# The end of the last image in a deformable-attention and bottleneck kernel: rows dealt by a product, a convolution by chunks, and depthwise steps on two engines

## The chip, the cores and the metric

The kernel runs on one core of a Trainium2 chip. The metric is the device time of one execution in microseconds (us). Three runs of the kernel before gave 3307.5, 3316.93 and 3306.41 us; the median is 3307.5 us. All data are 32-bit floats.

The engines are named as in the profile: PE (TensorE, matrix products, with PEld for its weight loads), DVE (VectorE), ACT (ScalarE), POOL (GpSimd) and SP (SyncE, which here only issues DMAs).

## What is computed

Eight images of 512 channels and 64x64 pixels pass through two layers. Each layer normalises its input over 32 groups of channels and adds its output to its input.

```python
# layer 0: deformable attention, 8 heads of 64 channels
q = einsum('oc,bchw->bohw', w_q, gn(x))
off = tanh(w_off2 @ gelu(q[..., ::4, ::4] * w_off1 + b_off1)) * 4
k, v = split(w_kv @ grid_sample_bilinear(q, grid + off))     # 16x16 = 256 keys
out = softmax((q * 0.125) @ k.T) @ v
x = x + w_out @ out + b_out

# layer 1: bottleneck
y = conv_w @ gn(x) + conv_b                       # 512 -> 32 channels
y = depthwise 3x3, stride 2 (y) + dw_b            # 64x64 -> 32x32
y = fc2_w @ (fc1_w @ y + fc1_b) + fc2_b           # 1024 -> 256 -> 1024 pixels
y = depthwise transposed 3x3, stride 2 (y) + de_b # 32x32 -> 64x64
x = x + out_w @ y + out_b                         # 32 -> 512 channels
```

## The kernel before

An image is held as 8 tiles of 512 pixels; a tile has 4 chunks of 128 channels on 128 partitions. The loop at L1101 goes over 256 rounds (image, tile, chunk) and 6 more. In a round, PE computes logits of the next round, weighted values and sums of exponentials of this one, and the output projection of the round 6 back (`LAG`), so that projection, residual add and statistics trail the attention. Work of layer 1 of the image before and of layer 0 of the next one is woven in by generators. All of it stands under a manual schedule: on each engine, the order of the code is the order of the instructions.

What happens behind the last attention round, in the code's names:

- `sum_exps` (L618) adds up the exponentials with a 0/1 matrix into the PSUM tile `pn`. `invert` (L637) takes the reciprocal `rn` on DVE (L641), and four small DMAs on SP (L647) copy rows of `rn` to other partitions[...].
- `scale_two` (L650) spreads a row of `rn` over its head's partitions by a shuffle (L654) and multiplies the weighted values with it (L656).
- `project_out` (L664) multiplies a tile with `wout`, 128x64 column tiles in pairs, 8 products for one chunk of output (L670). DVE then adds bias and residual (L677) and takes the statistics of the chunk (L680).
- `load_residual` (L658) and `store` (L682) are DMAs on SP.
- After the 6 trailing rounds, `layer1_last` (L991) runs `layer1` (L733) for the last image with nothing beside it: statistics over all chunks by `group_stats` (L164), whose power -0.5 is on POOL (L185); the convolution weights `cw` scaled by it (L746); the convolution `py` (L753), where each of four row blocks of an image uses 32 columns of PE; the same weights applied to the means (`pb`, L771), for the bias; copies by ACT into the padded map `y` in `wbuf` (L765); the bias added by DVE (L780); three row copies between blocks (L782); nine taps of the first depthwise step on DVE (L798, L800); transposes `pz`, the two linear steps `ph`, `pht`, `pu`; the map `u` (L864); the 18 tap operations of `upsample` on DVE (L884, L886) into `v`.
- `project_last` (L952) forms 32 output products of 128x512 in up to 6 PSUM banks at a time. For 24 of them DVE adds them to the residual (L983); for 8, ACT evicts (L980) and POOL adds (L981). Each is stored by its own DMA of 256 KB on SP (L986).

PSUM pools: `ps_s` has two buffers of two banks, `ps_a` the two banks `pa` and `pn`, `ps_mm` two banks.

Of the kernel before, what the change touches and what calls it, by code (L numbers as in the profile page):

```python
# [8 lines left out]
F32 = mybir.dt.float32  # L9
# [7 lines left out]
P = 128  # L17
# [32 lines left out]
def kernel(  # L50
# [45 lines left out]
    def spot(b, k):  # L96
        j = region[b]
        k %= NT + 1
        return spares[j] if k == 0 else regions[j][:, :, (k - 1) * TP : k * TP]
# [7 lines left out]
    def out_tile(b, t):  # L107
        return spot(b, t - 1)
# [40 lines left out]
    def col(k, n=1):  # L149
        return vec[:, k : k + n]  # L150
# [4 lines left out]
    def drain(*gens):  # L155
        for gen in gens:
            for _ in gen:
                pass
# [502 lines left out]
            xs[place[b]][:, oc : oc + n, t * TP : (t + 1) * TP],  # L661
        )

    def project_out(b, t, oc, st):  # L664

        ao, xt = q_tile(b, t), out_tile(b, t)
        pp = ps_mm.tile([P, TP], F32, tag="mm", name=f"pp_{b}_{t}_{oc}")
        for hp in range(NCC):
            for r in (0, DH):
                nc.tensor.matmul(  # L670
                    pp[r : r + DH, :],
                    wout[:, hp, oc * P + r : oc * P + r + DH],
                    ao[:, hp, :],
                    start=(hp == 0),
                    stop=(hp == NCC - 1),
                )
        nc.vector.scalar_tensor_tensor(  # L677
            xt[:, oc, :], pp, col(V_BOUT + oc), xt[:, oc, :], ALU.add, ALU.add
        )
        nc.vector.bn_stats(st[:, oc, t, :], xt[:, oc, :])  # L680
# [4 lines left out]
    def attention_max(b, t):  # L685

        qt = q_tile(b, t)
        for hp in range(NCC):
# [40 lines left out]
                    )  # L729
            nc.scalar.copy(qt[:, hp, :], pa)  # L730


    def layer1(b, st, project, place, v):  # L733

        w2 = {}
        for half in range(2):
# [4 lines left out]
                    fc2_wT[oc * P : (oc + 1) * P, half * 2 * NK : (half + 1) * 2 * NK],  # L741
                )

        gs = yield from group_stats(st, 1, b)
        cw = small.tile([P, NCC, CB], F32, tag="cw", name=f"cw_{b}")
        nc.vector.tensor_mul(cw, convw, gs[:, 1].unsqueeze(2).to_broadcast([P, NCC, CB]))  # L746
        yield None

        py = [ps_mm.tile([P, TP], F32, tag="mm", name=f"py_{b}_{h}") for h in range(2)]
        for h in range(2):  # L750
            for cc in range(NCC):
                for rb in range(4):
                    nc.tensor.matmul(  # L753
                        py[h][rb * CB : (rb + 1) * CB, :],
                        cw[:, cc, :],
                        out_tile(b, 2 * rb + h)[:, cc, :],
                        start=(cc == 0),
                        stop=(cc == NCC - 1),
                    )

        y = wflat[:, : (ROWS + 1) * (HW + 1)].rearrange("p (r c) -> p r c", c=HW + 1)
        nc.vector.memset(y[:, :, 0:1], 0.0)
        nc.vector.memset(y[0:CB, 0:1, :], 0.0)
        for h in range(2):
            nc.scalar.copy(  # L765
                y[:, 1 + 8 * h : 9 + 8 * h, 1:], py[h].rearrange("p (r c) -> p r c", c=HW)
            )
        pb = ps_mm.tile([P, TP], F32, tag="mm", name=f"pb_{b}")
        for cc in range(NCC):
            for rb in range(4):  # L770
                nc.tensor.matmul(  # L771
                    pb[rb * CB : (rb + 1) * CB, 0:1],
                    cw[:, cc, :],
                    gs[:, 0, cc : cc + 1],
                    start=(cc == 0),
                    stop=(cc == NCC - 1),
                )
        yb = small.tile([P, 1], F32, tag="yb", name=f"yb_{b}")
        nc.vector.tensor_sub(yb, col(V_CONVB), pb[:, 0:1])
        nc.vector.tensor_scalar_add(y[:, 1:, 1:], y[:, 1:, 1:], yb)  # L780
        for rb in range(1, 4):
            nc.vector.tensor_copy(  # L782
                y[rb * CB : (rb + 1) * CB, 0, 1:], y[(rb - 1) * CB : rb * CB, ROWS, 1:]
# [6 lines left out]
        o = (ROWS + 1) * (HW + 1)  # L790
        z = wflat[:, o : o + NK]
        z3 = z.rearrange("p (i j) -> p i j", j=32)
        for k in range(9):
            ki, kj = divmod(k, 3)
            yk = y[:, ki : ki + 15 : 2, kj : kj + 63 : 2]
            w = col(V_DWW + k)
            if k == 0:
                nc.vector.tensor_scalar(z3, yk, w, col(V_DWB), ALU.mult, ALU.add)  # L798
            else:
                nc.vector.scalar_tensor_tensor(z3, yk, w, z3, ALU.mult, ALU.add)  # L800
# [69 lines left out]
        def upsample(h, a):  # L870

            for c in range(2):
# [7 lines left out]
                for n, (k, dr, dc) in enumerate(taps):  # L880
# [4 lines left out]
                    else:  # L885
                        nc.vector.scalar_tensor_tensor(vk, uk, w, vk, ALU.mult, ALU.add)  # L886

        for h, a in ((0, 0), (0, 1), (1, 0)):
            upsample(h, a)
            yield None  # L890
# [97 lines left out]

        return project

    def layer1_last(b, st, other):  # L991
        return layer1(b, st, project_last(other), spot(other, 0), wbuf[:, 0:2, :])


    ROUNDS = NT * NCC
# [66 lines left out]
    with tc.manual_schedule():  # L1062
        load_x(0)
        load_wq()
        load_x(1)

        wkv = [es4[0:2], es4[2:4]]
        for i in range(2):
            for j in range(2):
                w = w_kvT.rearrange("(cc p) o -> p cc o", p=P)  # L1070
                nc.sync.dma_start(wkv[i][j], w[:, 2 * j : 2 * j + 2, i * C : (i + 1) * C])
        load_weights_late()
        st = new_stats(0, 0)
        drain(norm_x(0, st))

        shared = [wout[:, i, :].rearrange("p (k o) -> p k o", k=2) for i in range(3)]
        shared += [kt[:, 0:2, :], kt[:, 2:4, :], wout[:, 3, :]]
        drain(norm_q(0, st, norms))

        st = new_stats(0, 1)  # L1080
        blocks, other = norm_x(1, st), norm_q(1, st, norms)
        for n, step in enumerate(make_q(0, shared)):
            if n >= 3 * NCC and next(blocks, "end") == "end" and n >= 10 * NCC:
                next(other, None)
        drain(other)
        other = make_q(1, shared)
        next(other)
        rest.pop(0)()
        room = 0
        for step in samples[0]:  # L1090
            room += 6 if step is None else 2
            while room > 0:
                room -= next(other, 6) or 6
        drain(other)
        rest.pop(1)()
        next(samples[1])
        load_wout()
        project_k(0, mqs.pop(0), wkv[0])
        logits(*names[0])
        project_v(0, wkv[1])  # L1100
        for g in range(len(names) + LAG):  # L1101
            b, r = divmod(g, ROUNDS)
            if r == 0 and b < B:
                beside = next_image(b)
                st1s[b] = new_stats(1, b)

            def fill(room):
                while room > 0:
                    done = next(beside, None)
                    if done is None:  # L1110
                        break
                    room -= done

            summed = g % 2 == 0 and 0 <= g - 1 < len(names)
            if g % 2 == 0:
                scale_two()
            if g < len(names):
                weighted_values(*names[g])
            if summed:
                sum_exps(*names[g - 1])  # L1120
            if g < len(names):
                add_exps(*names[g])
            if r == Q_ROUND and 0 < b < B - 1:

                tiles = [free_es.pop(0) for _ in range(3)]
                made = make_q(b + 1, room_for_sums(tiles), lambda: invert(*names[g - 1]))
                while next(made) != LATE:
                    pass
                free_es.extend(tiles)
                logits(*names[g + 1])  # L1130
                drain(made)
                rest.pop(b + 1)()
            else:
                if summed:
                    invert(*names[g - 1])
                if g + 1 < len(names):
                    logits(*names[g + 1])
            if g % 2:
                scale_two()
            phase[0] = 0  # L1140
            if r >= LAG:
                fill(200)
            if g - LAG >= 0:
                ob, ot, oc = names[g - LAG]
                project_out(ob, ot, oc, st1s[ob])
            k = g + 1 - LAG
            if 0 <= k < len(names) and k % NCC < 2:
                load_residual(*names[k + k % NCC], 2)
            if k >= NCC and k % NCC == 2 and names[k - NCC][0] < B - 1:
                store(*names[k - NCC][:2])  # L1150
            phase[0] = 1
            if r >= LAG - 1:
                fill(200)
            if b + 1 < B:
                if r == ROUNDS - 2:
                    drain(beside)
                    project_k(b + 1, mqs.pop(b + 1))
                if r == ROUNDS - 1:
                    project_v(b + 1)
        drain(layer1_last(B - 1, st1s.pop(B - 1), B - 2))  # L1160


    halves = wflat[:, :P]
# [115 lines left out]
```

## Time and profile before

| what | value |
|---|---|
| span of the profiled execution | 3305.2 us |
| its own time | 3307.08 us |
| median of the three runs | 3307.5 us |
| PE busy | 3218.6 us (97%) |
| DVE busy | 2317.6 us (70%) |
| ACT busy | 1185.6 us (36%) |
| POOL busy | 603.5 us (18%) |
| mean granted PE clock | 0.989 |

Times in the profile count from the first instruction. A group is a line of the code on one engine; "idle before" is how long that engine stood still ahead of it. The chain of waits follows the work that ended last back to the start. PEclk is the granted PE clock as a share of full speed. The profiled execution lies 1.88 us under its own time, which includes what is before and after the span.

### The profile page before, as it was taken

What the parts mean: (1) busy time and instruction counts of PE and PEld (TensorE: products, weight loads), DVE (VectorE), ACT (ScalarE), POOL (GpSimd) and SP (SyncE); (2) the same over time, 40 slices, a digit from 0 to 9 for tenths busy, and PEclk for the clock granted to TensorE, in tenths of its full rate; (3) what the DMA queues carried; (4) which work ended last, traced back from release to release, by engine and by line L of the source; (5) the groups of instructions that cost most, each with busy time, mean ns of one, the idle gap of its engine ahead of it and who ended that gap; (6) DMA issues with size and microseconds to landing.
All of it is one profiled execution on the core that took longest, in us unless ns stands there. A gap on an engine that the chain in (4) does not pass through costs nothing.

```text
span 3305.2 us, 46114 instructions
## 1 busy us (share of the span) xinstructions
PE 3218.6 (97%) x18196; PEld 1532.4 (46%) x18196; DVE 2317.6 (70%) x3666; ACT 1185.6 (36%) x1641; POOL 603.5 (18%) x576
## 2 busy tenths in 40 slices
PE   6999999999999999999999999999999999999996
PEld 5884223348332583326733276322853238433222
DVE  7874765776758767587665977668776687757564
ACT  2343333343333433344333443334433244333420
POOL 1130300130402204022030211203021040300201
PEclk9999999999999999999999999999999999999996
DMA  7232222672327533284333833258233482422713
GB/s 277 74 93 76 75 78 65 202 154 76 114 82 221 125 90 90 91 225 114 103 96 114 205 98 108 78 181 177 68 103 90 176 178 65 122 70 74 132 47 121
DMA packets 293874, 390.62 MB, mean 118 GB/s; under 512 B 18320, under 2 KB 157840, under 8 KB 293648
## 3 DMA queue, kind: packets, MB, share of 16 engines
q1 hardware_dynamic: 240368, 261.72, 24.7%
q0 software_dynamic: 53280, 125.86, 17.4%
q8 instruction: 145, 2.38, 0.3%
q14 instruction: 81, 0.66, 0.1%
HBM read 193.52 MB, written 192.94 MB: 117 GB/s over the span
## 4 chain that ended last, share of the span: by engine, by line
PE 92%; DVE 5%; issue 1%; DMA 1%; ACT 0%; SPq 0%; POOL 0%; DVEq 0%; POOLq 0%; ACTq 0%
PE pp L670 27%; PE pq L275 22%; PE ps L583 14%; PE pa L601 13%; PE pn L628 4%; PE pqt L324 4%; PE po L896 2%; PE py L753 2%; PE pk L536 2%; PE pv L563 2%; DMA rn<-rn 1%; DVE st L201 1%; DVE rn L641 0%; PE po L428 0%; DVE wbuf L800 0%
## 5 line engine op out<-in xcount | busy, mean ns | idle before, releaser
L670 PE MATMUL pp<-image,wout 128*64 128x512 f32 x3584 | 828.1, 604 | 10.0 <-DVE image L656 8.3
L591 ACT ACTIVATE es<-ps 128x1024 f32<-128x1024 f32 x512 | 502.0, 1022 | 273.5 <-PE ps L583 211.3
L670 PEld LDWEIGHTS pp<-image,wout 128*64 128x64 f32 x3584 | 238.5, 137 | 561.0 <-issue 462.3
L601 PE MATMUL pa<-es,vt 128*64 128x512 f32 x2048 | 488.5, 598 | 1.7 <-ACT es L591 1.7
L275 PE MATMUL pq<-image,wbuf 128*128 128x256 f32 x2048 | 477.0, 381 | 1.9 <-DVE image L217 1.9
L677 DVE SCALAR_TENSOR_TENSOR image<-pp,vec,image 128x512 f32<-128x512 f32 x224 | 167.4, 747 | 426.0 <-PE pp L670 425.6
L522 POOL DMA_INDIRECT g<-qd,row x256 | 272.2, 1063 | 1032.1 <-DVE row L478 849.6
L583 PE MATMUL ps<-image,kt 64*64 64x512 f32 x3584 | 436.9, 602 | 0.0
L275 PEld LDWEIGHTS pq<-image,wbuf 128*128 128x128 f32 x2048 | 381.4, 191 | 56.2 <-issue 5.0
L608 ACT COPY image<-pa 128x512 f32<-128x512 f32 x224 | 132.1, 590 | 706.2 <-PE pa L601 706.2
L613 DVE TENSOR_TENSOR es<-es,es 128x1024 f32<-128x1024 f32 x256 | 310.6, 1213 | 71.4 <-PE pa L601 71.4
L601 PEld LDWEIGHTS pa<-es,vt 128*64 128x64 f32 x2048 | 137.5, 137 | 298.0 <-issue 278.0
L583 PEld LDWEIGHTS ps<-image,kt 64*64 64x64 f32 x3584 | 114.5, 132 | 306.6 <-issue 175.7
L334 ACT COPY qr<-pqt 128x512 f32<-128x512 f32 x224 | 131.2, 586 | 336.2 <-PE pqt L324 320.8
L641 DVE RECIPROCAL rn<-pn 128x512 f32<-128x512 f32 x64 | 214.7, 3355 | 9.4 <-PE pn L628 5.8
L185 POOL TENSOR_TENSOR gs<-ve,nhalf 128x4 f32<-128x4 f32 x16 | 16.7, 1041 | 1064.3 <-DVE ve L184 1064.3
L654 DVE STREAM_SHUFFLE rb<-rn 128x512 f32<-128x512 f32 x256 | 187.5, 732 | 0.1
L275 PE MATMUL pq<-es,es 128*128 128x256 f32 x768 | 181.5, 379 | 0.0
L948 POOL DMA_DIRECT2D out_dram<-part x126 | 137.9, 1324 | 153.9 <-ACT part L943 146.6
L201 DVE BATCH_NORM_STATS2 st<-image 128x6 f32<-128x512 f32 x256 | 158.8, 678 | 7.5 <-DMA image<-in_x_dram 7.4
L680 DVE BATCH_NORM_STATS2 st<-image 128x6 f32<-128x512 f32 x224 | 155.6, 695 | 7.7
L656 DVE TENSOR_TENSOR image<-image,rb 128x512 f32<-128x512 f32 x224 | 155.1, 692 | 7.8
(197 smaller groups left out, 3475.2 us busy)
## 6 DMA issues: line engine op xcount, KB each, us to landing
qd<-qr SPq DMA_DIRECT2D x256, 256.0 KB
image<-in_x_dram SPq DMA_DIRECT2D x112, 512.0 KB
out_dram<-image SPq DMA_DIRECT2D x49, 1024.0 KB
image<-in_x_dram POOLq DMA_DIRECT2D x48, 1024.0 KB
out_dram<-part POOLq DMA_DIRECT2D x126, 256.0 KB
image<-in_x_dram SPq DMA_DIRECT2D x16, 1024.0 KB
wbuf<-in_w_kvT_dram SPq DMA_DIRECT2D x14, 1024.0 KB
out_dram<-spare POOLq DMA_DIRECT2D x56, 256.0 KB
```

What stands on the lines that cost most here:

```text
L201: nc.vector.bn_stats(st[:, cc, t, :], x_tile(b, t)[:, cc, :])
L275: nc.tensor.matmul(bank[:, o * 2 * P : (o + 1) * 2 * P], w[:, k, o * P : (o + 1) * P], xh[:, k, :], start=(k == 0), stop=(k == 1),)
L522: nc.gpsimd.indirect_dma_start(held[-1][:, i, :, :].rearrange("p j d -> p (j d)"), None, qd[:, :], bass.IndirectOffsetOnAxis(ap=row[:, ky, ...
L583: nc.tensor.matmul(ps[k : k + DH, a, :], kt[r : r + DH, hp, kc * P + k : kc * P + k + DH], qt[r : r + DH, hp, :], start=True, stop=True,)
L591: nc.scalar.activation(e, ps, AF.Exp)
L601: nc.tensor.matmul(pa[a * DH : (a + 1) * DH, :], vt[:, kc, hd * DH : (hd + 1) * DH], es[kc][:, a, :], start=(kc == 0), stop=(kc == 1),)
L613: nc.vector.tensor_add(es[0], es[0], es[1])
L641: nc.vector.reciprocal(rn, denominators.pop((b, t)))
L654: nc.vector.stream_shuffle(rb, rn, [2 * (hp % 2) + hp // 2] * 32)
L670: nc.tensor.matmul(pp[r : r + DH, :], wout[:, hp, oc * P + r : oc * P + r + DH], ao[:, hp, :], start=(hp == 0), stop=(hp == NCC - 1),)
L677: nc.vector.scalar_tensor_tensor(xt[:, oc, :], pp, col(V_BOUT + oc), xt[:, oc, :], ALU.add, ALU.add)
L680: nc.vector.bn_stats(st[:, oc, t, :], xt[:, oc, :])
```

## The change

It touches only what follows the last attention round, for the last image. The other images, and the path taken when logits are too large, keep their order.

- The 6 trailing rounds are written out. The reciprocal's rows are dealt out by a product: POOL makes a 0/1 matrix `deal` (one memset, four copies), PE multiplies it with `rn` into the PSUM tile `rows`, and the shuffles read `rows`. The four DMAs are gone.
- ACT makes ten 128x128 diagonal matrices of depthwise weights in freed exponential buffers.
- The projection of the last tile is followed chunk by chunk by the statistics of the chunk before (`mean`) and the scaled convolution weights of the one before that (`scale`), called between the third and the fourth pair of its products. The convolution runs chunk by chunk.
- The bias is added in the eviction of the convolution, one half by ACT, one by DVE.
- Of the nine taps of the first depthwise step, DVE keeps five; PE does four with diagonal weights into `pd`, and DVE adds `pd`.
- In the upsampling, DVE keeps the even rows; PE does the odd rows in 12 products, and ACT evicts them with the bias.

```diff
-    def project_out(b, t, oc, st):
+    def project_out(b, t, oc, st, between=None):
...
+            if between:
+                between(hp)
...
+    def convolve(b, py, cw, h, cc):
+        for rb in range(4):
+            nc.tensor.matmul(
+                py[rb * CB : (rb + 1) * CB, :],
+                cw[:, cc, :],
+                out_tile(b, 2 * rb + h)[:, cc, :],
...
+    def last_tile(b, st):
...
+        def mean(cc):
+            c = slice(cc, cc + 1)
+            nc.vector.bn_aggr(mv[:, cc, :], st[:, cc].rearrange("p t s -> p (t s)"))
+            nc.tensor.matmul(gps[0][:, c], group, mv[:, cc, 0:1], start=True, stop=True)
+            nc.vector.tensor_copy(gs[:, 0, c], gps[0][:, c])
+            nc.vector.tensor_sub(dv[:, c], mv[:, cc, 0:1], gs[:, 0, c])
+            nc.vector.tensor_mul(dv[:, c], dv[:, c], dv[:, c])
+            nc.vector.tensor_add(dv[:, c], dv[:, c], mv[:, cc, 1:2])
+
+        def scale(cc):
+            c = slice(cc, cc + 1)
+            nc.tensor.matmul(gps[1][:, c], group, dv[:, c], start=True, stop=True)
+            nc.vector.tensor_scalar_add(ve[:, c], gps[1][:, c], EPS)
+            nc.gpsimd.tensor_tensor(gs[:, 1, c], ve[:, c], nhalf[:, c], ALU.pow)
+            nc.vector.tensor_scalar(cw[:, cc, :], convw[:, cc, :], gs[:, 1, c], None, ALU.mult)
+
+        def between(oc):
+            def step(hp):
+                if hp == 2 and oc >= 2:
+                    scale(oc - 2)
+                if hp == 2 and oc >= 1:
+                    mean(oc - 1)
+
+            return step
+
+        for oc in range(NCC):
+            project_out(b, t, oc, st, between(oc))
...
+        convolve(b, py[:, 0, :], cw, 0, 0)
+        scale(2)
+        convolve(b, py[:, 1, :], cw, 1, 0)
+        convolve(b, py[:, 0, :], cw, 0, 1)
+        mean(3)
+        convolve(b, py[:, 1, :], cw, 1, 1)
+        scale(3)
+        for cc in range(NCC - 1):
+            convolve_mean(pb, cw, gs, cc)
+        for h in range(2):
+            convolve(b, py[:, h, :], cw, h, 2)
+        convolve_mean(pb, cw, gs, 3)
+        for h in range(2):
+            convolve(b, py[:, h, :], cw, h, 3)
...
+        if conv:
...
+            py, pb = conv()
+            nc.vector.tensor_sub(yb, col(V_CONVB), pb)
+            for h in range(2):
+                to, fr = y[:, 1 + 8 * h : 9 + 8 * h, 1:], py[h].rearrange("p (r c) -> p r c", c=HW)
+                if h:
+                    nc.vector.tensor_scalar_add(to, fr, yb)
+                else:
+                    nc.scalar.activation(to, fr, AF.Identity, bias=yb)
...
+            if diag and k > 4:
+                nc.tensor.matmul(pd, diag[V_DWW + k], yk, start=(k == 5), stop=(k == 8))
+                if k == 8:
+                    nc.vector.tensor_add(z, z, pd)
...
+        if diag:
+
+            for h, tag in enumerate(("pa", "pn")):
+                upsample(h, 0)
+                pv = ps_a.tile([P, TP], F32, tag=tag, name=f"pv_{b}_{h}")[:, : 2 * P]
...
+                    for n, (k, dr, dc) in enumerate(taps):
+                        nc.tensor.matmul(
+                            rows[:, :, c::2],
+                            diag[V_DEW + k],
+                            u[:, 4 * h + dr : 4 * h + dr + 4, dc : dc + 32],
...
+                nc.scalar.activation(
+                    v[:, h, :].rearrange("p (r c) -> p r c", c=HW)[:, 1::2, :],
+                    rows,
+                    AF.Identity,
+                    bias=col(V_DEB),
+                )
+            yield from project(b, v, [lambda: None])
+            return
...
-        for g in range(len(names) + LAG):
+        for g in range(len(names)):
...
-        drain(layer1_last(B - 1, st1s.pop(B - 1), B - 2))
+
+        b, t, st = B - 1, NT - 1, st1s.pop(B - 1)
+        sum_exps(*names[-1])
+
+        deal = es4[3][:, 1, :P]
+        nc.gpsimd.memset(deal, 0.0)
+        for q in range(4):
+            nc.gpsimd.tensor_copy(
...
+        rn = small.tile([P, TP], F32, tag="rn", name="rn_last")
+        nc.vector.reciprocal(rn, denominators.pop((b, t)))
+
+        diag = {}
...
+            nc.scalar.activation(diag[w], ident, AF.Copy, scale=col(w))
+        project_out(b, t - 1, 2, st)
+        rows = ps_s.tile([P, 2, TP], F32, tag="s", name="rn_rows")[:, 0, :]
+        nc.tensor.matmul(rows, deal, rn, start=True, stop=True)
+        project_out(b, t - 1, 3, st)
+        for hp in range(NCC):
+            rb = small.tile([P, TP], F32, tag="rb", name=f"rb_last_{hp}")
+            nc.vector.stream_shuffle(rb, rows, [2 * (hp % 2) + hp // 2] * 32)
+            ao = q_tile(b, t)[:, hp, :]
+            nc.vector.tensor_mul(ao, ao, rb)
+        for oc in (0, 2):
+            load_residual(b, t, oc, 2)
+        drain(layer1_last(b, st, b - 1, lambda: last_tile(b, st), diag))
```

## The prediction

> **What bounds the kernel now.** I read the page first: busy shares and the 40 slices say where time could come from at all.
>
> ```profile
> PE   6999999999999999999999999999999999999996
> PEclk9999999999999999999999999999999999999996
> ```
>
> TensorE is busy in 38 of 40 slices. Only the first and the last slice (82 us each) have slack, and the change touches only what follows the last image's last attention round. So the gain is bounded by the last 100 us; of them the final 24 us are stores. Next I asked for the stages of that end (us in the stretch; busy time of PE, weight load, DVE, ACT, POOL; granted clock; DMA share; GB/s).
>
> ```profile
> 3218.00:3222.00 4.00, 2.16 (x8) 0.42 (x8) 3.85 (x7) 0.00 (x0) 0.00 (x0) 1.00 0.97 344
> 3222.00:3225.40 3.40, 1.38 (x6) 0.40 (x8) 2.86 (x7) 0.00 (x0) 0.00 (x0) 1.00 1.04 365
> 3225.40:3228.80 3.40, 3.40 (x10) 0.97 (x8) 1.45 (x2) 0.00 (x0) 0.00 (x0) 0.51 0.44 148
> ...
> 3242.40:3249.20 6.80, 5.04 (x25) 1.17 (x28) 0.60 (x4) 0.00 (x0) 1.03 (x1) 0.51 0.00 0
> 3249.20:3254.00 4.80, 4.80 (x76) 1.57 (x68) 0.00 (x0) 0.70 (x2) 0.00 (x0) 0.99 0.02 3
> ...
> 3256.10:3275.00 18.90, 8.84 (x62) 4.18 (x62) 11.72 (x35) 1.06 (x2) 0.08 (x1) 0.50 0.00 0
> 3275.00:3290.20 15.20, 14.57 (x49) 7.10 (x48) 13.49 (x24) 3.44 (x5) 7.51 (x6) 0.50 0.84 314
> ```
>
> The reader sees two things: the clock halves in three stretches, each after PE stood idle; and from 3275 the DMA share is 0.84 and more, so the last stage is bound by its own stores. Then the chain of waits, in order of time:
>
> ```profile
> 3210.69 3.34 DVE rn L641
> ...
> 3215.92 1.69 DMA rn<-rn
> ...
> 3224.35 0.70 DVE image L656
> ...
> 3242.81 1.04 POOL gs L185
> 3243.87 0.29 DVE cw L746
> ...
> 3244.22 9.64 PE py L753 x64
> 3253.89 0.60 ACT wbuf L765
> 3254.51 0.77 DVE wbuf L780
> ```
>
> The chain is serial from here: reciprocal, row DMA, scaling of tile 7, projection (ends 3238.20), statistics, convolution (ends 3253.86), nine taps, bottleneck, upsampling, stores. Last the SP queue:
>
> ```profile
> 3275.70 10.72 SPq L986 DMA_DIRECT2D out_dram<-image  x16
> 3295.83 3.41 SPq L986 DMA_DIRECT2D out_dram<-image  x3
> ```
>
> Stores go out from 3275.70 to 3299.24. So end = first store + 29.5 us, and only what moves the first store counts, plus a little from gaps in the DMA share.
>
> [...] halved 3225.4 to 3228.8 (3.4 us) and 3242.4 to 3249.2 (twice that), then from 3256.1 on. A window with PE at 1.38 of 3.40 was followed by half rate, 2.16 of 4.00 was not; my estimate of the limit is 40 to 50% busy. [...] scalings and L677 adds alternate as the code issues them. [...] Between L628's 32-column and L670's 64-column tiles I see no gap beyond 0.1 us, so I charge nothing. [...] L677, with a PSUM input, took 0.75.
>
> **The change part by part**, on the profiled execution (span 3305.2, time 3307.08, so 1.88 us lie around it; the median shown, 3307.5, stands 0.4 above).
>
> **A, rows dealt by a product.** The four DMAs and their 1.69 us landing go. The reciprocal still ends at 3214.03. The product is one 128x128x512 matmul: two passes of 0.43 us (the spacing of L670's records), 3214.1 to 3215.0. But it is queued ahead of project_out of tile 6, chunk 3, whose 3.46 us then end at 3218.5 instead of 3217.27; and the shuffles now come after that chunk's add and statistics on DVE (0.75 + 0.65, to 3220.0). Four pairs of shuffle and multiply at 1.50 us (3217.76 to 3219.26): the last ends at 3226.05 against 3225.05, so 1.0 us later. POOL's five small operations (0.2 us memset at the start of the kernel; 0.1 to 1.0 each for the rest) lie beside the 3.34 us reciprocal; at the high end the product comes 1.4 us later. ACT's ten diagonals (about 0.3 each, L825 is 0.37) have nothing behind them until the convolution. SP has three fewer issues; w2, residual and w1 loads are needed at 3227 or later. Against the 1.0: before, half a clock cost 1.7 us of continuous work (3225.4 to 3228.8); now that window falls partly into waits. I take 1.0 of it back (ends 0 and 1.7). Sum 0 (-0.7 to +2.4).
>
> **B, statistics inside the projection.** Five small matmuls at 0.37 (L173) = 1.85 us. And a new wait: after chunk 2's third pair PE holds scale(0), then mean(1). mean(1) waits for DVE's aggregate, which is queued behind the weight scaling, which waits for POOL's power. Before's own chain prices it: from gpsb's end 3242.47 over add 0.17, POOL 1.04 and weights 0.29 (0.17 for a quarter) to the aggregate (0.26) and the issue, 2.0 us. PE stands still, and chunk 2's (then 3's) last pair and all after it is queued behind. Twice: 4.0. Sum +5.85.
>
> **C, convolution by chunks.** Gone: 3238.20 to 3244.22, 6.0 us of add, statistics, group products and power. The convolution at full clock is 16 x 0.43 = 6.9 us (image 0's, 596.42 to 603.31); three small matmuls 1.1, the bias products 0.45, and mean(3) waits once more, about 0.5, since two 0.86 us groups stand before it. 9.0 against 9.64. Sum -6.6.
>
> **D, from the convolution to the end of the taps.** Before 6.7 us (3253.86 to 3260.56). Now the bias is in the eviction, and the second half goes by DVE alone: 0.7; row copies 0.6; five taps 0.45 + 4 x 0.52; adding the PSUM share 0.46 (L864): 4.4 with gaps. PE's four 256-column taps are 0.43 each at full clock, 0.85 at half: done in 1.9 or 3.6 us beside DVE's 3.1, at worst 0.5 late. Sum -2.3 (-1.8 at half clock).
>
> **E, the bottleneck's matmuls (no edit).** They take 0.66 + 1.97 + 1.08 + 2.18 us at half clock; image 0 shows 0.44, 1.07, 0.63 and 1.19 at full: up to 2.55 back. PE is idle about 1.8 us after its taps and then under half busy, so I expect the clock to drop midway: -1.1 (0 to -2.55).
>
> **F, upsampling.** Before, 18 DVE operations, 3268.85 to 3274.89, 6.07 us to the first add of L983. Now DVE does 6 (2.1 us), PE 12 taps of 128 columns before any output product. The nearest row is by_pixel's transposes of that size, 0.116 us per pass at full clock: two passes each, 2.8 us, then a group of four output products, 0.86, and latency: 3.95 us. At half clock 5.4 + 1.75 + 0.15 = 7.3. PE is busy through all of it, so the clock may return midway: I take 6.3. Sum +0.2 (-2.1 to +1.25).
>
> **G, the stores.** 32 of 256 KB; at the 383 GB/s of the best slices 21.9 us against 23.5 of issue. A full PE clock closes some of the early gaps: -0.5 (0 to -1.2).
>
> Sum: 0 + 5.85 - 6.6 - 2.3 - 1.1 + 0.2 - 0.5 = -4.45; 3307.5 - 4.5 = 3303.0 us.
>
> **The rivals.** *The clock stays up* (A -0.7, E -2.55, F -2.1, G -1.2): -9.6, 3298. For it: PE now has work in the taps and the upsampling, where before it stood idle for 6.6 and 4.1 us. Against: two gaps of 1.8 to 2.0 us remain, and 1.38 of 3.40 was too little. *The waits of B don't come*, if the queues are not in the order of the code: 4.0 less, 3299. Against: DVE's order in the trace is that of the code everywhere I looked within the loop. *Slower: the two waits of B halve the clock.* They leave windows as little as 40% busy at 3236 to 3243; then the convolution starts cold and needs one or two windows to recover, 1.7 to 3.4 us, the late taps cost 0.5, and PE, which now carries the upsampling, stays cold there (+1.25), with E and G at 0 and A at +1.0: 1.0 + 5.85 - 6.6 + 3.4 - 1.8 + 1.25 = +3.1, 3310.5; it decides once more than 4.5 us are lost to the half clock. If the whole convolution ran cold, 3.6 more: 3314.
>
> **How the numbers follow.** Forecast 0.50, clock up 0.25, no waits 0.08, slower 0.17. The range reaches from beyond the clock-up case to the cold one: 3296 to 3311; the likeliest case's own is 3300 to 3306. What can be told from no change is 0.3%, 9.9 us: under 3297.6 lie somewhat less than half of the clock-up case and half of the no-waits case, with a rest for costs I mis-sized, 0.19; above 3317.4 only the cold case's far end and unforeseen waits, 0.07.
>
> **What would show it.** A: the last L656 multiply about 1 us later, no DMA on rn. B: two PE gaps of 2 us that end with VectorE's aggregate. C: convolution end near 3253. D: taps end 4.4 us after it. E, F: granted clock between 3255 and 3270. G: first store near 3272, end 29 us after it. I am wrong if the gaps are absent, if the clock stays at 1.00 through the upsampling, or if rounds before 3209 change their length.

## The result

Over 14 runs of each, the changed kernel took 3304.02 us (median; 3291.71 to 3317.68), the kernel before 3307.72 us (3299.86 to 3316.93). The ratio is 0.9993, with a 95% interval of 0.9983 to 1.0003: no difference that this measurement can tell from none. In microseconds the interval goes from 5.6 less to 1.0 more, so the gain of 4.45 us that was forecast (3303.0 us) lies inside it, and so does no gain at all.

A single time says little here. The rounds ahead of the change move by as much as the change is worth: the reciprocal of the fifth tile of image 6 (the images are counted from 0) starts 3.1 us later in the profile after than in the profile before, that of image 4's fifth tile 1.4 us earlier, and nothing there was edited. A second profile of the kernel before differs from the first by as much, as shown below. So I count from a mark that both kernels share, the start of the last sum of exponentials (the last group of L628). From there to the end of the span:

| event, us from the mark | before | after | change of the step that ends here |
|---|---|---|---|
| last multiply by the dealt rows ends | 15.86 | 17.15 | |
| add of tile 7's chunk 0 starts | 17.63 | 18.34 | +0.71 (A) |
| add of tile 7's chunk 3 starts | 29.04 | 34.48 | +4.73 (B) |
| convolution ends | 44.63 | 43.90 | -6.17 (C) |
| transposes start | 51.48 | 49.19 | -1.56 (D) |
| map u done | 59.63 | 57.08 | -0.26 (E) |
| first output add starts | 65.74 | 62.55 | -0.64 (F) |
| end of the span | 96.02 | 90.99 | -1.84 (G) |

A minus sign means that the step got shorter, as in the prediction. "Tail" below is the time from the mark to the end of the span. It is 5.03 us shorter; the span is only 2.9 us shorter, since its mark came 2.13 us later.

The stages of the end, in the profile after (same columns as in the prediction; the stretches are cut about where the clock changes):

```profile
3221.50:3227.00 5.50, 2.96 (x8) 0.82 (x10) 5.24 (x13) 0.00 (x0) 0.00 (x0) 0.69 0.88 276
3227.00:3235.70 8.70, 8.45 (x40) 2.66 (x38) 5.41 (x13) 0.00 (x0) 0.00 (x0) 1.00 0.44 152
3235.70:3243.70 8.00, 5.10 (x26) 2.09 (x24) 3.43 (x12) 0.00 (x0) 1.12 (x2) 1.00 0.00 0
3243.70:3247.10 3.40, 3.40 (x14) 0.56 (x14) 1.91 (x6) 0.00 (x0) 0.00 (x0) 0.55 0.00 0
...
3255.20:3260.80 5.60, 2.43 (x11) 1.62 (x10) 4.11 (x10) 0.69 (x1) 0.00 (x0) 1.00 0.00 0
3260.80:3271.30 10.50, 8.13 (x63) 5.47 (x62) 3.66 (x13) 0.37 (x1) 0.00 (x0) 0.51 0.01 2
3271.30:3278.00 6.70, 6.04 (x37) 3.14 (x35) 4.14 (x7) 2.52 (x5) 2.00 (x2) 1.00 0.38 143
```

Up to the first output products the granted clock is at 0.50 in three places again: while the rows are spread over the last tile (3223.55 to 3226.95), for 3.4 us behind the second of the new waits (3244.03 to 3247.43), and from the transposes into the upsampling (3261.09 to 3271.33). It comes back to 1.00 in the upsampling, where PE is busy without a gap from 3268.45 to 3272.75.

The timeline of the profile after around the first of the new waits (start, duration, engine, line; in brackets the idle time before it and what ended it):

```profile
3236.00 0.38 PE L777 MATMUL pn_last<-dv_last,cst 128*128 128x1 f32 x2
3236.42 0.16 DVE L778 TENSOR_SCALAR ve_last<-pn_last 128x1 f32<-128x1 f32 x1 [1.39 <-PE pn_last L777]
3236.66 0.58 POOL L779 TENSOR_TENSOR gs_last<-ve_last,nhalf 128x1 f32<-128x1 f32 x1 [23.37 <-DVE ve_last L778]
3237.28 0.24 DVE L780 TENSOR_SCALAR cw_last<-convw,gs_last 128x32 f32<-128x32 f32 x1 [0.70 <-POOL gs_last L779]
3237.43 0.36 DVE L768 BATCH_NORM_AGGREGATE mv_last<-st 128x2 f32<-128x48 f32 x1
3237.85 0.38 PE L769 MATMUL pa_last<-mv_last,cst 128*128 128x1 f32 x2 [1.46 <-DVE mv_last L768]
```

This is step B as it was written: PE stands still for 1.46 us before the mean's product, since the aggregate is queued behind the weight scaling and that waits for POOL. The part that differs most is POOL's power: 0.58 us for one column, where I took the 1.04 us that it needed for four before.

The same view at the end of the convolution:

```profile
3255.27 0.69 ACT L836 ACTIVATE wbuf<-py_last,yb 128x512 f32<-128x512 f32 x1 [43.76 <-PE py_last L736]
3255.99 0.75 DVE L834 TENSOR_SCALAR wbuf<-py_last,yb 128x512 f32<-128x512 f32 x1 [2.28 <-ACT wbuf L836]
3256.78 0.59 DVE L859 COPY wbuf<-wbuf 32x64 f32<-32x64 f32 x3
3256.80 2.13 PE L876 MATMUL pd<-wbuf,es 128*128 128x256 f32 x8 [1.60 <-DVE wbuf L834]
```

Both halves are evicted after the last product (it ends at 3255.2), one behind the other. I had them side by side: this is what step D lacks.

### The profile page after: what moved, and what is told of

It is laid out like the page before. It is cut to its first block, busy times and chain, and to the rows that moved or that the text cites. A ratio compares the mean times of both kernels' runs of the same rounds, so it can differ in the third digit from the quotient of the medians.

```text
span 3302.3 us, 46222 instructions
## 1 busy us (share of the span) xinstructions
PE 3225.7 (98%) x18242; PEld 1538.2 (47%) x18242; DVE 2315.2 (70%) x3669; ACT 1190.5 (36%) x1652; POOL 606.0 (18%) x584
## 4 chain that ended last, share of the span: by engine, by line
PE 92%; DVE 5%; issue 1%; ACT 0%; DMA 0%; SPq 0%; POOL 0%; ACTq 0%; DVEq 0%; POOLq 0%
PE pp L670 27%; PE pq L275 22%; PE ps L583 14%; PE pa L601 13%; PE pn L628 4%; PE pqt L324 4%; PE po L1006 2%; PE pk L536 2%; PE pv L563 2%; PE py L736 1%; DVE st L201 1%; DVE rn L641 0%; PE po L428 0%; DMA rn<-rn 0%; DVE mq L286 0%
```

## The experiments

Ten kernels ran, nine of them edits of the changed kernel. All numbers count from the mark unless they stand in a view. Each has one profile, and the last two were also timed in rounds. The kernel before, profiled twice, shows how far single profiles can be trusted: its two tails differ by 1.95 us, 0.85 of it ahead of the first output add and 1.10 behind it.

**Shuffles ahead of tile 6's chunk 3.** The four pairs of shuffle and multiply move up by one statement.

```diff
+        for hp in range(NCC):
+            ...
         project_out(b, t - 1, 3, st)
-        for hp in range(NCC):
-            ...
```

> All times here count from the start of the last sum of exponentials (line L628's last group), where the kernel before needs 96.0 us to the end of the span and the changed one 91.0. Edit: the four pairs of shuffle and multiply stand ahead of the projection of tile 6, chunk 3. Theory (the product pays nothing because its shuffles are queued behind that chunk's add and statistics): the last multiply ends near 12.3 instead of 17.15, the first chunk of tile 7 near 13.1 instead of 18.3, PE has no gap over 0.5 us there and its clock stays at 1.00; the tail is 5 to 5.5 us shorter, near 85.7. Rival (the residual loads or the PSUM bank held by the late add take the place of the wait): the chunk ends at 15 or later and the tail is shortened by less than 3 us.

The last multiply ended at 12.16, the add of chunk 0 started at 13.71 instead of 18.34, the tail took 86.42 us instead of 90.99, a gain of 4.6 where I had expected 5 to 5.5. The timeline of this run:

```profile
3209.78 1.10 PE L1290 MATMUL rn_rows<-rn_last,es 128*128 128x512 f32 x2 [0.35 <-DVE rn_last L1282]
...
3210.80 8.56 PE L670 MATMUL pp<-image,wout 128*64 128x512 f32 x38
3210.92 0.01 DVE L1293 LOAD_MASK_SELECT rb_last<-rn_rows  x1
...
3216.86 0.74 DVE L679 SCALAR_TENSOR_TENSOR image<-pp,vec,image 128x512 f32<-128x512 f32 x1
```

The shuffles run beside chunk 3's products, PE goes from tile 6 into tile 7 without a gap, and the add that was moved back (3216.86) holds nobody up. The theory stands. In the kernel before, the last multiply ended at 15.86, so with this order the product pays, and with the order of the change it does not. No run has the four DMAs together with this order. In the kernel before the rows let the first shuffle start 8.56 us after the mark, and four pairs of 1.50 us would end near 14.6 (an estimate), against 12.16 here.

**Mean before scale.** Inside the projection, the two calls change places.

```diff
-                if hp == 2 and oc >= 2:
-                    scale(oc - 2)
                 if hp == 2 and oc >= 1:
                     mean(oc - 1)
+                if hp == 2 and oc >= 2:
+                    scale(oc - 2)
```

> Counted from the start of the last sum of exponentials; the changed kernel needs 91.0 us from there. Edit: within the projection of tile 7, the mean of one chunk is taken before the scale of the chunk ahead of it. Theory (VectorE's aggregate waits behind the weight scaling, which waits for POOL, and this both stalls PE and halves its clock): both gaps of 1.45 us ahead of the mean's product vanish, the clock stays at 1.00 up to the convolution; the projection's last add starts near 30.7 instead of 34.5, the convolution ends near 39.7 instead of 43.9, tail near 86.8. Rival (the gaps are lost, but the clock drops all the same): only 2.9 us, tail 88.1. Second rival (the scale's wait moves to the chunk's add and from there to a PSUM bank): under 1.5 us.

Chunk 3's add started at 30.85, the convolution ended at 39.11 instead of 43.90, the tail took 86.48 us. The timeline of this run, at the same place as above:

```profile
3236.10 0.38 PE L769 MATMUL pa_last<-mv_last,cst 128*128 128x1 f32 x2
3236.34 0.36 PE L777 MATMUL pn_last<-dv_last,cst 128*128 128x1 f32 x2
...
3236.63 3.65 PE L670 MATMUL pp<-image,wout 128*64 128x512 f32 x16
```

No idle time stands before either product. Two gaps, 2.9 us, account for most of the 3.6 us at chunk 3; the rest, and 1.2 us in the convolution, fits the half clock, which did not come behind these products here: the granted clock was 1.00 from 3227.1 to 3257.8, while in the changed kernel it was 0.50 for 3.4 us from 3244.03 on.

**Fillers in PE's gaps.** Seven products of `ident` with `wout` into a free bank, read by nobody: three of 256 columns behind the taps, one of 128 behind the transposes and behind `ph`, two of 256 behind `pu`.

```diff
+        def fill(*cols):
+            ...
+                nc.tensor.matmul(pf[:, :n], ident, wout[:, 0, :n], start=True, stop=True)
...
                 if k == 8:
+                    fill(256, 256, 256)
                     nc.vector.tensor_add(z, z, pd)
```

> Counted from the start of the last sum of exponentials; the changed kernel needs 91.0 us from there. Edit: seven products whose result nobody reads (128x128 weights, 256 or 128 columns) are put into PE's gaps between the taps of the first depthwise step and the upsampling. Theory (PE's idle time there halves the clock, and the half clock costs 2 us in the bottleneck and 1.5 us in the upsampling): the granted clock stays at 1.00 from the convolution to the first output products; from the transposes to the map u 5.8 us instead of 7.9, from u to the first output add 4.0 instead of 5.5; tail near 87.5. Rival (the clock falls for another reason, or the fillers delay the products behind them by as much): tail 90.5 to 91.5.

The stages of this run, from the taps to the stores:

```profile
3250.00:3255.60 5.60, 3.89 (x19) 2.55 (x16) 4.10 (x10) 0.69 (x1) 0.00 (x0) 1.00 0.00 0
3255.60:3261.20 5.60, 4.93 (x58) 2.98 (x57) 1.83 (x8) 0.37 (x1) 0.00 (x0) 1.00 0.00 0
3261.20:3265.70 4.50, 4.44 (x36) 3.45 (x36) 1.83 (x6) 0.95 (x2) 0.00 (x0) 1.00 0.02 5
3265.70:3284.00 18.30, 14.34 (x60) 5.05 (x56) 16.99 (x31) 5.50 (x8) 10.15 (x8) 1.00 0.93 347
```

The clock stayed at 1.00 to the last output product. Transposes to u took 5.58 us instead of 7.89, u to the first add 4.54 instead of 5.47; the fillers delayed the transposes by 0.2. The first output add came 3.2 us sooner. The tail took 88.39: 0.9 less gain than I expected, most of it lost in the stores. From the first add to the end it took 29.0 us, against 28.44 in the changed kernel, although the last add was done at 76.97 instead of 81.90. So the stores set that time, not the adds.

**Upsampling by VectorE alone.** `if diag:` ahead of PE's odd rows becomes `if diag and False:`.

> Counted from the start of the last sum of exponentials; the changed kernel needs 91.0 us from there. Edit: the upsampling goes back to VectorE alone, 18 operations; everything else of the change stays. Theory (PE's share of the upsampling gains little by itself, but brings PE's clock back in time for the output products, and that closes the early gaps of the stores): from the map u to the first output add 6.1 us instead of 5.5; from there to the end 30.2 instead of 28.4; tail near 93.4. Rival (the stage of stores is faster for another reason, such as where the output products' banks stand): 28.4 stays, tail near 91.6.

From u to the first add 6.10 us, from there 29.19, tail 92.31: 1.3 us over the changed kernel, about half of the 2.4 expected. The granted clock stayed at 0.50 from the transposes (3255.1) to the last output product. SP's first 16 issues in this run:

```profile
3269.18 10.69 SPq L1096 DMA_DIRECT2D out_dram<-image  x16
```

They took 9.97 us in the changed kernel, so 0.7 us of step G goes with the clock, which is at 1.00 there in the changed kernel (3271.33 to 3278.0). The rest of its 1.84 does not.

**Statistics in one go.** The projection of tile 7 runs undisturbed, then four aggregates, two group products, one power, one weight scaling, as before the change; the convolution keeps its order.

```diff
-            project_out(b, t, oc, st, between(oc))
+            project_out(b, t, oc, st)
+        for cc in range(NCC):
+            nc.vector.bn_aggr(mv[:, cc, :], st[:, cc].rearrange("p t s -> p (t s)"))
+        nc.tensor.matmul(gps[0][:, :NCC], group, mv[:, :, 0], start=True, stop=True)
...
+        nc.vector.tensor_mul(cw, convw, gs[:, 1].unsqueeze(2).to_broadcast([P, NCC, CB]))
```

> Counted from the start of the last sum of exponentials; the changed kernel needs 91.0 us from there. Edit: the projection of tile 7 runs undisturbed and the statistics of all four chunks follow it in one go, as before the change; the convolution keeps its order by chunks, the rest of the change stays. Theory (the chunked statistics pay nothing as they stand, since their two waits, five extra products and the half clock after the second wait eat the 6 us they save): the last add of the projection near 28.8 instead of 34.5, the convolution's end at 43.5 to 44.6 against 43.9, tail 90.6 to 91.7. Rival (chunking is worth several us even so): convolution's end at 46 or later, tail over 93.

Chunk 3's add started at 28.62, the convolution ended at 44.43, the tail took 90.96 us against 90.99. The chunked statistics, as the change orders them, are worth 0.5 us at the convolution's end. The first output add came 0.4 us sooner without them (62.15 against 62.55), and the last three issues of SP, which vary with no edit, as the next run but one shows, took 3.22 us instead of 2.15. I see no gain from them beyond the convolution.

**Rows by DMA.** The product and `deal` go, the four DMAs on `rn` come back; the shuffles stay behind chunk 3.

```diff
-        nc.tensor.matmul(rows, deal, rn, start=True, stop=True)
+        for a in range(2):
+            for i in range(2):
+                to, fr = DH * a + CB * (1 - i) + 2 * i, DH * a + CB * i + 2 * i
+                nc.sync.dma_start(rn[to : to + 2, :], rn[fr : fr + 2, :])
```

> Counted from the start of the last sum of exponentials; the changed kernel needs 91.0 us from there. Edit: the rows of the reciprocal go back to four DMAs on SP; the shuffles stay where the change puts them, behind the add and the statistics of tile 6's chunk 3. Theory (the product costs PE 1.1 us ahead of that chunk and nothing waits for the rows any more, since the shuffles are queued behind the chunk in either case): the last multiply ends 1.3 to 1.5 us sooner, near 15.7, tail 89.5 to 90.3. Rival (the DMAs' landing is what held the shuffles): the last multiply at 17 or later, tail 91 or more.

The timeline of this run:

```profile
3226.01 2.43 SPq L1283 DMA_DIRECT2D rn_last<-rn_last  x4
...
3229.26 0.75 DVE L679 SCALAR_TENSOR_TENSOR image<-pp,vec,image 128x512 f32<-128x512 f32 x1 [1.95 <-PE pp L670]
3230.05 0.69 DVE L682 BATCH_NORM_STATS2 st<-image 128x6 f32<-128x512 f32 x1
3230.67 0.01 DVE L1288 LOAD_MASK_SELECT rb_last<-rn_last  x1
```

The first shuffle has no idle time before it: it follows the statistics at once, and the rows are there. The last multiply ended at 15.53, the tail took 89.57 us, 1.4 less than with the product. The first output add came 1.5 us sooner as well (61.05). With the change's order, the product is a loss.

**The kernel before, once more.** No edit.

> No edit: the kernel before, profiled once more. It tells what of the two profiles is chance. Counted from the start of the last sum of exponentials, the first profile has 65.7 us to the first output add and 30.3 from there to the end. Theory (the tail repeats itself to some tenths of a microsecond while the rounds ahead of it move by several; and of the 1.8 us by which the changed kernel's stores are faster, 1.25 lie in the last three issues of SP, 3.41 us against 2.15, which no edit touches): first add at 65.5 to 66.0, the last three issues near 2 us, from first add to end near 29.1, tail near 94.8. Rival (the 3.4 us belong to the kernel before, whose stores run at the half clock): 30.3 and 96.0 again.

First add at 64.89, outside the half microsecond that I allowed: the convolution ended 0.84 us sooner than in the first profile. Its stretches of half clock lay elsewhere as counted from the mark, which I take for the cause: the granted clock had a mean of 0.67 from 8.1 to 18.1 us and of 0.61 and 0.54 in the two stretches of 4 us from 31.1 to 39.1, where the first profile has 0.50 from 16.3 to 19.7 and from 33.3 to 40.1. The mark itself came 1.75 us later, with no edit. From first add to end 29.18, tail 94.07. SP's queue in the profile after, and in this repetition:

```profile
3274.64 9.97 SPq L1096 DMA_DIRECT2D out_dram<-image  x16
...
3293.62 2.15 SPq L1096 DMA_DIRECT2D out_dram<-image  x3
```

```profile
3276.60 10.73 SPq L986 DMA_DIRECT2D out_dram<-image  x16
...
3296.73 2.02 SPq L986 DMA_DIRECT2D out_dram<-image  x3
```

The 3.41 us of the last three issues, shown in the prediction, did not come again; in the twelve profiles they lie between 1.96 and 3.41 us with no edit that explains it. The first 16 issues do repeat: they took 10.7 us in the three profiles where the output adds start at half clock (both of the kernel before, and the one with VectorE's upsampling), and 10.0 in the nine where they start at full clock (the first eight output products took 2.09 us in the three, 1.14 in the nine). Against this profile the change shortens the tail by 3.1 us, against the first by 5.0.

**Two PSUM tiles for the convolution.**

```diff
-        py = ps_s.tile([P, 2, TP], F32, tag="s", name=f"py_{nm}")
+        py = [ps_s.tile([P, 2, TP], F32, tag="s", name=f"py_{nm}")[:, 0, :]]
+        py.append(ps_mm.tile([P, TP], F32, tag="mm", name=f"py1_{nm}"))
```

> Counted from the start of the last sum of exponentials; the changed kernel needs 91.0 us from there. Edit: the two halves of the last image's convolution get PSUM tiles of their own instead of the two banks of one tile. Theory (ScalarE waits for the last product into the tile, not for its own half, and VectorE's eviction of the other half then waits for ScalarE): ScalarE starts about 0.3 us before the convolution's end instead of behind it, VectorE follows within 0.8 us of the convolution's end, from the convolution's end to the transposes 4.6 us instead of 5.3, tail near 90.3. Rival (ScalarE waits for the bias): no change.

The timeline of this run:

```profile
3255.28 0.69 ACT L837 ACTIVATE wbuf<-py_last,yb 128x512 f32<-128x512 f32 x1 [42.85 <-PE py_last L736]
3255.46 0.59 PE L736 MATMUL py_last<-spare,cw_last 128*32 128x512 f32 x1
...
3256.14 0.75 DVE L835 TENSOR_SCALAR wbuf<-py_last,yb 128x512 f32<-128x512 f32 x1 [1.56 <-PE py_last L736]
```

ACT now starts ahead of the other half's last products, and DVE waits for PE instead of ACT: 4.64 us to the transposes instead of 5.29. The place is as the theory has it. The tail is not: 90.96. Transposes to u gained 0.44 more, but u to the first add took 6.08 instead of 5.47: the clock was at 0.50 from about 3262.2 to about 3272.4, so most of PE's upsampling ran cold. At the first output add 0.54 us of gain was left. It is missing at the end because the last three issues took 3.16 us instead of 2.15, and those vary with no edit, as the repetition above shows.

**Both orders mended.** The first two edits together.

> Edit: both orders mended, shuffles ahead of tile 6's chunk 3 and mean ahead of scale; nothing else. Counted from the start of the last sum of exponentials. Theory (the two gains are of different places and add up, 4.6 us and 4.5 us): tail near 82 instead of 91.0 (before: 96.0), so about 14 us or 0.42% less than the kernel before, ratio 0.9958. Rival (both were the same clock, so the second gives little): tail 85 or more, ratio 0.9967 or more.

Tail 80.13 us, convolution's end at 34.15 instead of 43.90. The tail is 10.9 us shorter, 1.8 more than the two gains added up. Up to the convolution's end they do add up: 9.75 us against 4.95 and 4.79. From there to the first output add it took 17.51 us, against 18.65 in the changed kernel and 18.89 and 18.85 in the two runs with one edit each, which makes 1.6 of the 1.8. PE's products were faster there: 0.73 us for `pht` and 4.36 for the upsampling, against 1.06 and 5.40 in the run with the shuffles moved up and 1.06 and 5.36 in the mean-first run. I take that for less half clock in this stage; the granted clock was 0.50 for 10.2 us of it in each of those two runs. In five rounds the ratio to the kernel before was 0.9958 (0.9945 to 0.9972); the medians were 3305.4 us here and 3317.7 us for the kernel before, timed again beside it.

**All of it.** Both orders, two PSUM tiles, and the fillers, the third of them cut to 128 columns.

> Edit: as b1_order, and the two halves of the convolution in PSUM tiles of their own, and seven unread products that fill PE's gaps between the taps and the upsampling. Counted from the start of the last sum of exponentials. Theory: 0.7 us from the eviction (ScalarE no longer waits for the other half) and 3 us from the clock on top of b1_order, tail near 78.5, about 17.5 us less than before, ratio 0.9947. Rival (the fillers stand in the way[...], and the eviction waits for something else): not better than b1_order.

The tail took 77.42 us. The stages of this run, from the mark to the last output product:

```profile
3219.60:3228.00 8.40, 8.05 (x40) 2.41 (x40) 8.12 (x11) 0.17 (x1) 0.76 (x5) 1.00 0.00 0
3228.00:3233.00 5.00, 5.00 (x24) 1.49 (x22) 4.74 (x9) 0.00 (x0) 0.00 (x0) 1.00 0.74 232
3233.00:3245.50 12.50, 12.50 (x66) 4.39 (x62) 8.07 (x29) 0.00 (x0) 1.13 (x2) 1.00 0.47 160
3245.50:3253.70 8.20, 8.17 (x102) 2.66 (x94) 3.16 (x13) 0.69 (x1) 1.09 (x2) 1.00 0.01 2
3253.70:3258.30 4.60, 3.51 (x18) 2.36 (x14) 4.09 (x10) 0.00 (x0) 0.00 (x0) 1.00 0.00 0
3258.30:3264.00 5.70, 4.97 (x59) 3.06 (x59) 1.84 (x8) 0.38 (x1) 0.00 (x0) 1.00 0.00 1
3264.00:3268.50 4.50, 4.44 (x36) 3.46 (x37) 1.83 (x7) 0.95 (x2) 0.00 (x0) 1.00 0.02 4
3268.50:3286.00 17.50, 14.39 (x62) 5.08 (x58) 16.86 (x31) 5.50 (x8) 10.16 (x8) 1.00 0.92 345
```

PE is at full clock all the way and nearly without gaps to the convolution's end. The ratio to the kernel before was 0.9941 (0.9916 to 0.9966). It overlaps with that of the orders alone; only the tails, 77.4 and 80.1, and the first output adds, 48.97 and 51.66, tell the two apart, with one profile each. Both beat the kernel before by their times, and the changed one (90.99) by the tail.

## Why the prediction was right

The measured time alone shows little. Its medians differ by 3.7 us, close to the forecast of 4.45, but its interval holds no change too, and so did the forecast's range of 3296 to 3311. The tail says more: it got shorter by 5.0 us against the first profile of the kernel before and by 3.1 against the second, on both sides of the forecast. That the total came so close is partly luck, since the steps miss in both directions. Of the steps (where the two profiles of before differ, the second value is against the repetition):

- **A**, forecast 0, was +0.71 or +0.27. The mechanism is the one foreseen: the last multiply came 1.3 us later (1.0 forecast), and 0.6 or 1.0 came back (1.0 forecast), because the half clock (0.50 to 3226.95) was over before the last products of chunk 0, which wait for that multiply (to 3228.46) and start at 3228.52. In the kernel before they start at 3225.10, and the clock was 0.50 from 3225.45 to 3228.85. The rows-by-DMA run puts the product at a loss of 1.4 to 1.6 us in this order, and the moved-up shuffles turn that into a gain of 4.6. I had seen that order and priced it, but not that mending it is worth about as much as the whole change.
- **B**, forecast +5.85, was +4.73 or +5.65. Both waits came where they were put, at 1.46 and 1.44 us instead of 2.0; the term mis-sized is POOL's power, 0.55 to 0.58 us for one column instead of 1.04. The half clock behind the second wait (0.50 for 3.4 us), which I had given to the slower rival, took part of that back: chunk 3's last pair needed 1.87 us against 1.08 in the mean-first run.
- **C**, forecast -6.6, was -6.17 or -5.81. A, B and C together were forecast at -0.75 and measured at -0.73 or +0.11, so the close agreement with the first profile is luck. The run with the statistics in one go says the same without my sums: nothing gained beyond the convolution.
- **D**, forecast -2.3, was -1.56. The failed term is "the second half goes by DVE alone: 0.7": DVE waited for ACT, and ACT for the whole tile. The two-tile run shows 0.65 of the missing 0.74.
- **E**, forecast -1.1, was -0.26: the clock dropped at the transposes (to 0.50 at 3261.09; they start at 3260.50), not midway. The far end of 2.55 was real: with fillers the stage took 5.58 us, 2.57 less than before.
- **F**, forecast +0.2, was -0.64, and -1.57 with the clock held: inside the stated ends.
- **G**, forecast -0.5, was -1.84 or -0.74. The difference of 1.1 between the two profiles of before is chance; the 0.7 that is left goes with the clock at the first output adds (0.50 before, 1.00 after).

D and E together gained 1.6 us less than forecast, F and G 2.2 or 1.1 us more.

The rival with the clock up did not come by itself, but the fillers show that its mechanism is real. The rival without waits came only when the order was changed. The slower rival's half clock did set in behind the second wait, at 0.50 for 3.4 us; by the mean-first run it cost about 1.9 us (0.7 in the projection, 1.2 in the convolution), too little to decide.

One of the signs of being wrong did show, that rounds ahead of 3209 change their length. They do so in the repetition of the kernel before as well, so the change is not their cause.

What stays open: why the last stores of some runs take up to 1.4 us longer, how busy PE must be for its clock to stay at 1.00, and what the four DMAs would do with the shuffles moved up.

## What to carry to other kernels

When work is woven into a busy engine's queue, ask of each inserted instruction what its producer is queued behind on its own engine; here the order of two calls cost 4.5 us and the place of one loop 4.6, each about as much as the whole change brought (5.0 or 3.1). In a serial tail with PE half idle, look at the granted clock as well: here the transposes to u took 5.58 us with PE's gaps filled and the clock at 1.00, and 7.89 us without, with the clock at 0.50 from 3261.09 on. And where runs vary by more than the change, time it from a mark inside the trace, and profile the unchanged kernel twice before reading single profiles closely.

## What the runs showed of the hardware that was not expected

- POOL's power took 1.04 us for 128x4 elements and 0.54 to 0.58 us for 128x1: three columns more cost nearly 0.5 us.
- In the profiles before and after, the granted clock ahead of the first output product went to 0.50 for 3.4 us (3225.45 to 3228.85 before; 3223.55 to 3226.95 and 3244.03 to 3247.43 after) or for two or three times as long (3242.51 to 3249.33 before; 3261.09 to 3271.33 after), but for the last drop before, at 3256.17, which lasted into the output products (to 3290.29).
- The clock fell to half at 3244.03 in the profile after, though PE counted as busy for 1.97 of the 3.41 us before it (58%; 3.41 us is a third of the 10.24 us at half clock from 3261.09 on), more than the 40 to 50% that I had estimated as the limit from two stretches of the profile before. In the run with the shuffles moved up it fell after 1.95 busy us (3223.75 to 3227.16) and stayed up after 1.97 (3230.58 to 3233.99), so the busy share of the profile does not decide it alone. How much work keeps the clock up is not settled by these runs.
- The clock stayed at half behind more work than it had once stayed up with. In the profile after, two stretches at half clock with PE busy for 2.55 and 2.59 of 3.41 us (from 3261.09 and 3264.50) were followed by another one; it came back behind the third, with 2.87.
